# Reordering the last two sequences of a token router, and routing the last one by halves, in a two-layer state-space, attention and mixture-of-experts kernel

## The chip, the cores and the metric

The kernel runs on one NeuronCore of a Trainium2 chip, in one launch. The metric is the device time of that launch in microseconds (us). TensorE (PE) does the matrix products and writes PSUM; its weight loads are shown apart (PEld). VectorE (DVE) and ScalarE (ACT) do elementwise work and reductions, GpSimd (POOL) constants and indirect transfers. Each engine runs its own instructions in order and waits on semaphores of the others. Transfers are issued from the queues of SyncE (SP), ACT and POOL.

## The reference, cut to what matters

The input `x` holds 8 sequences of 1024 tokens with 256 features. Two layers follow each other, each of the form `x = x + attention(norm(x)) + ffn(norm(x))`. The first attention is a state-space scan followed by a layer norm, a GELU and an output projection; the first feed-forward part is a grouped top-2 mixture of experts. The second layer is what the change touches:

```python
qkv = einsum('bsd,fd->bsf', x, w_qkv)          # one head
attention = softmax(attn_logits, axis=1)       # over an axis of length 1
out = einsum(attention, v) @ w_o.T             # so: sum of all tokens' values, for each sequence

logits = xt @ wg                               # 8192 tokens, 8 experts
topv, topi = top_k(softmax(logits), 2)
locs = cumsum(one_hot(topi.T)) - 1             # place of each choice in its expert, all first choices first
valid = pos < capacity                         # capacity 2048
disp[e, pos] += token                          # 8 experts: 256 -> 1024 -> 256, relu
out = sum(gate * y[topi, pos])
```

The place of a token in its expert depends on all tokens before it (and, for second choices, on all first choices), so the routing is a running count over the sequences, and no expert can start before the last token is routed.

## The kernel before, in words

P is 128. A tile is 128 tokens, a sequence is TPB = 8 tiles, NB = 8 sequences, NT = 64 tiles. The state-space scan and the first experts fill the first half of the launch. What is edited is the stage behind it, between the scan and the second layer's experts. For each sequence `b` it does this:

- `project` (L1012, L1019): 16 products per sequence on PE, in four PSUM tiles `pd` of two tiles each, and four additions on DVE of the residual `hb`. The result is the layer's output `y`, which goes to `out_dram` by an SP transfer (L1274) and is later added to there.
- `measure` (L178, L179): mean and variance of each tile on DVE. `roots` (L1030) or, for the last sequence, `scales` (L183 to L185): a square root on ACT, a reciprocal and a product on DVE.
- `normal_out` (L190): eight ACT instructions write the normalised rows `xs`. `normal_in` and `turn` (L933, L934) do the same for the scan output of the next sequence.
- `turn_out` (L1058, L1061): 16 transposes on PE into `pt` (three buffers), and four ACT copies to `xT`, which also sum the tokens into `sums`.
- `logits` (L1069, L1077, L1084, L1085): `xs` goes to the DRAM table `xd`, PE multiplies `xT` with the router weights, ACT copies the logits.
- `attend` (L1092 to L1099): the sum over the tokens times the folded value and output weights, one product pair into the single PSUM bank `pc`.
- `route` for `n` tiles at once (L1106 to L1197): maximum, exponential (ACT, L1112), two picks on DVE (`pick_two`, L200 to L214), counts by two PE products into `pc` (L1120), ACT copies `tot` (L1125), a running sum (L1128), places (L1138 to L1155), and then for both choices and each eight tiles one-hot matrices `hl` and `hh` on DVE (L1161, L1166, L1170), a scaling by the tile number on ACT for each tile (L1174) and a product on PE for each tile (L1176), which adds token numbers up in `pi[0]` and `pi[1]` over the whole launch. At the end the gate weights `w` go to `xd` (L1194).

Sequences are routed in pairs (16 tiles) up to 4 and 5, behind the step of the sequence after them; sequence 6 and sequence 7 are routed alone (8 tiles each). `ends` carries the running count from one `route` to the next.

Behind the last `route`, DVE turns `pi` into the list `invi` (L1327 to L1358), which says for each expert which rows of `xd` it takes. The experts (L1360 on) gather these rows with POOL (L1385), transpose them (L1399), do two products (L1416, L1434) and scatter with addition (L1446).

The source order is not the order of execution: a scheduler interleaves independent instructions of an engine when the program is built. Pools with few buffers (`pc` one, `pt` three, `pd` two, one-hot tiles two) add waits where a buffer is still in use.

Of the kernel before, what the change touches and what calls it, by code (L numbers as in the profile page):

```python
# [24 lines left out]
def kernel(  # L25
# [886 lines left out]
    with tc.tile_pool(name="xr", bufs=3) as xr, tc.tile_pool(name="tr", bufs=1) as tr, tc.tile_pool(  # L912
# [153 lines left out]
        def logits(b):  # L1066

            xs, xT, sums = moved[b][3:]
            nc.sync.dma_start(  # L1069
                xd[b * S : (b + 1) * S, :D].rearrange("(i p) d -> p i d", p=P), xs  # L1070
            )
            pr = ps_d.tile([P, 2, D], F32, name="pd")
            pr = pr.rearrange("p a d -> p (a d)").rearrange("p (t e) -> p t e", t=TPB)
            for t in range(TPB):
                n = 2 if t < TPB - 1 else 1
                for c in range(DC):
                    nc.tensor.matmul(  # L1077
                        pr[:, t : t + n, :],
                        lhsT=xT[:, c, t * P : (t + 1) * P],
                        rhs=wg_t[:, c, : n * (P // 2)],  # L1080
                        start=(c == 0),
                        stop=(c == DC - 1),
                    )
            nc.scalar.copy(logit[:, b % 2 * TPB : (b % 2 + 1) * TPB, :], pr[:, :, :E])  # L1084
            nc.vector.tensor_reduce(colsum[:, :, b], sums, AX.X, ALU.add)  # L1085
# [15 lines left out]
        def route(t0, n, last):  # L1101
# [54 lines left out]

            for j in range(2):
                for i in range(0, n, TPB):
                    some = slice(i, i + TPB)
                    hl = hotp.tile([P, TPB, P], BF16, name="hl")  # L1160
                    nc.vector.tensor_tensor(  # L1161
                        hl, bc(place, 1, [P, TPB, P]), bc(cutb[:, j, some], 2, [P, TPB, P]),
                        ALU.is_equal,
                    )
                    hh = hotp.tile([P, TPB, 2, P], BF16, name="hh")
                    nc.vector.tensor_tensor(  # L1166
                        hh[:, :, 1, :], bc(column[:, j, :], 1, [P, TPB, P]),
                        bc(cutf[:, j, some], 2, [P, TPB, P]), ALU.is_equal,
# [4 lines left out]
                    for t in range(TPB):  # L1173
                        nc.scalar.mul(hh[:, t, 1, :], hh[:, t, 1, :], float(t0 + i + t))  # L1174
                    for t in range(TPB):
                        nc.tensor.matmul(  # L1176
                            pi[j], lhsT=hl[:, t, :], rhs=hh[:, t],
                            start=(t0 + i + t == 0), stop=(t0 + i + t == NT - 1),
                        )
# [74 lines left out]
        for n in (TPB, 2 * TPB):  # L1254
            go_on[n] = r1.tile([P, 2, E, n + 1], F32, name=f"go_on{n}")
            nc.gpsimd.memset(go_on[n], 1.0)
            nc.gpsimd.memset(go_on[n][:, :, :, 0], 0.0)
# [12 lines left out]
        for b in range(NB):  # L1270
# [17 lines left out]
            if b < NB - 1:  # L1288
                measure(b, whole)
                if b:  # L1290
                    logits(last)
                roots(b)
                if b == 0:
                    add_first(1, firsts[1])
                    third = later_rows(2)
                if b == 1:
                    add_first(2, third)
            else:
                measure(b, slice(0, TPB // 2))
                logits(last)  # L1300
# [7 lines left out]
        b = NB - 1  # L1308
        mv, rstd, off = moved[b]
        for some in (slice(0, TPB // 2), slice(TPB // 2, TPB)):  # L1310
            if some.start:
                measure(b, some)
            scales(mv[:, 0, some], rstd[:, 0, some], off[:, 0, some])
            normal_out(b, some)
            turn_out(b, some)
            if not some.start:
                ends = route((b - 1) * TPB, TPB, ends)
        logits(b)
# [3 lines left out]
        ends = route(b * TPB, TPB, ends)  # L1322
# [172 lines left out]
```

## Time and profile before

The median of three runs is 1945.62 us (1943.92 to 1947.21). The profiled execution took 1946.52 us, and its span, from the first to the last instruction, 1944.8 us.

| engine | busy us of 1944.8 | share |
|---|---|---|
| PE | 1806.0 | 93% |
| PEld | 1369.1 | 70% |
| DVE | 707.8 | 36% |
| ACT | 715.4 | 37% |
| POOL | 668.0 | 34% |

A share of the whole span says little on a stage of 60 us in it. Between 952.8 and 1007.8 us, the stage of the last two sequences, DVE is the busy engine. The instructions of that stretch are read from the timeline of each engine, in which a line has the start, the duration and what the engine waited for; durations of neighbours overlap a little there, so the distance from start to start is the better measure of what an instruction costs. [...]

### The profile page before, as it was taken

To read this page: it belongs to the slowest core of one execution; us is meant where nothing else is said; L and a number is where in the kernel's file an instruction comes from. 1 tells how busy PE (TensorE), PEld (TensorE's weight loads), DVE (VectorE), ACT (ScalarE), POOL (GpSimd) and SP (SyncE) were. 2 spreads that over 40 slices of the span, in tenths; PEclk is the share of its full clock that TensorE was granted. 3 is DMA by queue.
4 is the path that set the end of the run, shared out by engine and by line. 5 is a ranking of instruction groups with operands and counts; after the bars stand their busy time and mean duration, and the time that the engine had idled before them with its cause. 6 is when DMAs were issued, how large, how long until landed. Compare 5 with 4: busy or idle time off the path is not lost.

```text
span 1944.8 us, 24219 instructions
## 1 busy us (share of the span) xinstructions
PE 1806.0 (93%) x8619; PEld 1369.1 (70%) x8619; DVE 707.8 (36%) x2121; ACT 715.4 (37%) x1625; POOL 668.0 (34%) x676
## 2 busy tenths in 40 slices
PE   6987789999999998789959999999999999999996
PEld 5876667788888887579836676667667666766764
DVE  6754688354454444687760010101001010100100
ACT  5972354233333321588932222222222222222221
POOL 0100001566666667111013344343333333333322
PEclk9987899899999999899969999999999999999998
DMA  9998422465556566699633465542323232232211
GB/s 267 231 190 178 106 61 83 120 187 161 175 177 174 164 185 190 217 303 230 164 114 55 64 123 80 102 63 61 63 34 82 39 77 41 61 61 35 39 17 22
DMA packets 226840, 233.16 MB, mean 120 GB/s; under 512 B 50904, under 2 KB 199200, under 8 KB 226592
## 3 DMA queue, kind: packets, MB, share of 16 engines
q0 software_dynamic: 65248, 98.68, 26.2%
q1 hardware_dynamic: 158784, 130.54, 23.5%
q10 hardware_dynamic: 2688, 2.40, 0.4%
q8 instruction: 68, 1.11, 0.2%
q14 instruction: 52, 0.43, 0.1%
HBM read 136.87 MB, written 97.85 MB: 121 GB/s over the span
## 4 chain that ended last, share of the span: by engine, by line
PE 52%; DVE 3%; ACT 2%; DMA 1%; issue 1%; POOL 0%; POOLq 0%; ACTq 0%; DVEq 0%
PE phe L1416 23%; PE poe L1434 22%; PE pd L1012 2%; PE px L1399 1%; PE pt L933 1%; PE pd L1077 1%; ACT y L190 1%; DMA out_dram<-yo,invi 1%; DVE st L178 1%; PE pi L1176 1%; DVE hb L977 0%; PE pt L1058 0%; ACT hh L1174 0%; DVE hl L1161 0%; PE pt L1220 0%
## 5 line engine op out<-in xcount | busy, mean ns | idle before, releaser
L1416 PE MATMUL phe<-xTe,w1t 128*128 128x512 f32 x1024 | 447.1, 595 | 0.6 <-DVE xTe L1400 0.6
L1434 PE MATMUL poe<-w2t,hT 128*128 128x256 f32 x2048 | 447.3, 379 | 0.0
L1434 PEld LDWEIGHTS poe<-w2t,hT 128*128 128x128 f32 x2048 | 386.9, 190 | 51.5 <-issue 0.5
L1416 PEld LDWEIGHTS phe<-xTe,w1t 128*128 128x128 f32 x1024 | 195.5, 191 | 233.5 <-issue 230.4
L1446 POOL DMA_INDIRECT out_dram<-yo,invi x128 | 201.8, 1576 | 446.0 <-DMA out_dram<-yo,invi 229.7
L1423 ACT ACTIVATE hT<-phe,b1T 128x512 f32<-128x512 f32 x256 | 175.9, 687 | 248.4 <-PE phe L1416 244.6
L1445 ACT ACTIVATE yo<-yo,gr 128x256 f32<-128x256 f32 x128 | 58.0, 500 | 441.4 <-DVE yo L1441 441.4
L1441 DVE TENSOR_TENSOR yo<-poe,b2t 128x512 f32<-128x512 f32 x64 | 44.2, 691 | 406.6 <-PE poe L1434 406.6
L1385 POOL DMA_INDIRECT xg<-xd,invi x128 | 124.5, 973 | 195.5 <-PE px L1399 90.2
L1400 DVE COPY xTe<-px 128x512 f32<-128x512 f32 x64 | 41.2, 686 | 383.5 <-PE px L1399 383.5
L814 POOL DMA_INDIRECT yr<-yo,goes x142 | 140.3, 988 | 65.6 <-DVE yo L811 27.7
L792 POOL DMA_INDIRECT xb<-xnd,choice x142 | 140.7, 991 | 46.9 <-issue 32.9
L322 PE MATMUL pk<-kr 128*128 128x129 f32 (+7 forms) x896 | 144.7, 298 | 9.7 <-ACT kr L333 9.0
L322 PEld LDWEIGHTS pk<-kr 128*128 128x128 f32 x896 | 125.2, 196 | 30.9 <-ACT kr L333 19.6
L263 PE MATMUL pgu<-xT,wb 128*128 128x256 f32 x568 | 142.2, 394 | 1.0 <-ACT xT L253 0.7
L263 PEld LDWEIGHTS pgu<-xT,wb 128*128 128x128 f32 x568 | 107.8, 196 | 27.6 <-ACT xT L253 13.2
L333 ACT COPY kr<-pk 128x256 f32<-128x256 f32 x192 | 70.0, 373 | 91.5 <-DVE kr L329 88.9
L268 ACT ACTIVATE sg<-pgu 128x256 f32<-128x256 f32 x87 | 33.3, 383 | 186.1 <-PE pgu L263 186.1
L278 PE MATMUL pd<-wb,hh 128*128 128x256 f32 x284 | 80.9, 399 | 5.5 <-DVE hh L271 5.4
L270 DVE TENSOR_TENSOR hh<-pgu,sg 128x256 f32<-128x256 f32 x87 | 36.8, 423 | 133.6 <-ACT sg L268 133.3
L811 DVE TENSOR_SCALAR yo<-pd,xb 128x256 f32<-128x256 f32 x142 | 62.4, 478 | 55.6 <-PE pd L278 54.5
L655 POOL DMA_DIRECT2D base<-y x8 | 12.7, 1582 | 192.8 <-ACT kr L333 56.2
(323 smaller groups left out, 2375.1 us busy)
## 6 DMA issues: line engine op xcount, KB each, us to landing
wb<-wpk SPq DMA_DIRECT2D x71, 384.0 KB, 3.5
xnd<-xr SPq DMA_DIRECT2D x32, 512.0 KB, 8.9
hk<-kscr SPq DMA_DIRECT2D x32, 512.0 KB, 4.7
hb<-yr POOLq DMA_DIRECT2D x10, 1024.0 KB, 12.1
base<-bout_t SPq DMA_DIRECT2D x8, 1024.0 KB, 7.8
base<-y POOLq DMA_DIRECT2D x8, 1024.0 KB, 9.8
hb<-base SPq DMA_DIRECT2D x8, 1024.0 KB, 14.2
out_dram<-y SPq DMA_DIRECT2D x8, 1024.0 KB, 11.5
```

Source lines behind the costliest of these rows:

```text
L263: nc.tensor.matmul(pgu[:, j, :], lhsT=gu[:, j, c, :], rhs=xT[:, c, :], start=(c == 0), stop=(c == DC - 1),)
L278: nc.tensor.matmul(pd[:, q, :], lhsT=hh[:, q * P : (q + 1) * P], rhs=wb[:, 2 * DC * I : WW], start=True, stop=True,)
L322: nc.tensor.matmul(pk[:, j, :n], lhsT=t[:, 1 - j, P:], rhs=t[:, j, P - k : P - k + n], start=True, stop=True,)
L333: nc.scalar.copy(t[:, :, P:], pk[:, :, k : k + P])
L792: nc.gpsimd.indirect_dma_start(out=xb[:, q, : D + 1], out_offset=None, in_=xnd[:, :], in_offset=bass.IndirectOffsetOnAxis(ap=choice[:, 2 * ...
L811: nc.vector.tensor_scalar(yo[:, q, :], pd[:, q, :], xb[:, q, D : D + 1], None, ALU.mult)
L814: nc.gpsimd.indirect_dma_start(out=next(yr_own)[:, :], out_offset=bass.IndirectOffsetOnAxis(ap=goes[:, 2 * n + q : 2 * n + q + 1], axis=0) ...
L1385: nc.gpsimd.indirect_dma_start(out=xg[:, q, :], out_offset=None, in_=xd[:, :], in_offset=bass.IndirectOffsetOnAxis(ap=invi[:, q0 + q : q0 ...
L1416: nc.tensor.matmul(ph, lhsT=w1t[:, c, h * P : (h + 1) * P], rhs=xT[:, c], start=(c == 0), stop=(c == DC - 1),)
L1423: nc.scalar.activation(hT[:, h], ph, AF.Relu, bias=b1T[:, e * HC + h : e * HC + h + 1])
L1434: nc.tensor.matmul(po[:, r, :], lhsT=hT[:, h, q + r, :], rhs=w2t[:, h, :], start=(h == 0), stop=(h == HC - 1),)
L1446: nc.gpsimd.indirect_dma_start(out=of[:, :], out_offset=bass.IndirectOffsetOnAxis(ap=invi[:, q0 + r : q0 + r + 1], axis=0), in_=yo[:, r, : ...
```

## The change

The loop over the sequences now ends at the last but one. Sequence 6 is normalised, transposed and given its logits before the last sequence is projected; it is then routed, and its attention term is made, before the last sequence is measured. The last sequence is measured and normalised in two halves of four tiles, and then each half is transposed, given logits and routed by itself (`route` with four tiles), the second half with the running count of the first. `logits` takes a range of tiles and writes that range of `xd`; `route` builds its one-hot tiles with a width `w` of four or eight. A constant tile for a running sum over four tiles is added.

```diff
@@ -1063,16 +1063,15 @@
                         AF.Copy, accum_out=sums[:, c, hf : hf + 1],
                     )
 
-        def logits(b):
+        def logits(b, some):
 
             xs, xT, sums = moved[b][3:]
-            nc.sync.dma_start(
-                xd[b * S : (b + 1) * S, :D].rearrange("(i p) d -> p i d", p=P), xs
-            )
+            rows = xd[(b * TPB + some.start) * P : (b * TPB + some.stop) * P, :D]
+            nc.sync.dma_start(rows.rearrange("(i p) d -> p i d", p=P), xs[:, some, :])
             pr = ps_d.tile([P, 2, D], F32, name="pd")
             pr = pr.rearrange("p a d -> p (a d)").rearrange("p (t e) -> p t e", t=TPB)
-            for t in range(TPB):
-                n = 2 if t < TPB - 1 else 1
+            for t in range(some.start, some.stop):
+                n = 2 if t < some.stop - 1 else 1
                 for c in range(DC):
                     nc.tensor.matmul(
                         pr[:, t : t + n, :],
@@ -1081,8 +1080,10 @@
                         start=(c == 0),
                         stop=(c == DC - 1),
                     )
-            nc.scalar.copy(logit[:, b % 2 * TPB : (b % 2 + 1) * TPB, :], pr[:, :, :E])
-            nc.vector.tensor_reduce(colsum[:, :, b], sums, AX.X, ALU.add)
+            t0 = b % 2 * TPB
+            nc.scalar.copy(logit[:, t0 + some.start : t0 + some.stop, :], pr[:, some, :E])
+            if some.stop == TPB:
+                nc.vector.tensor_reduce(colsum[:, :, b], sums, AX.X, ALU.add)
 
         def attend(b):
 
@@ -1154,25 +1155,26 @@
             cutf = rt.tile([P, 2, n], F32, name="cutf")
             nc.vector.tensor_copy(cutf, cut[:, 1])
 
+            w = min(n, TPB)
             for j in range(2):
-                for i in range(0, n, TPB):
-                    some = slice(i, i + TPB)
-                    hl = hotp.tile([P, TPB, P], BF16, name="hl")
+                for i in range(0, n, w):
+                    some = slice(i, i + w)
+                    hl = hotp.tile([P, TPB, P], BF16, name="hl")[:, :w]
                     nc.vector.tensor_tensor(
-                        hl, bc(place, 1, [P, TPB, P]), bc(cutb[:, j, some], 2, [P, TPB, P]),
+                        hl, bc(place, 1, [P, w, P]), bc(cutb[:, j, some], 2, [P, w, P]),
                         ALU.is_equal,
                     )
-                    hh = hotp.tile([P, TPB, 2, P], BF16, name="hh")
+                    hh = hotp.tile([P, TPB, 2, P], BF16, name="hh")[:, :w]
                     nc.vector.tensor_tensor(
-                        hh[:, :, 1, :], bc(column[:, j, :], 1, [P, TPB, P]),
-                        bc(cutf[:, j, some], 2, [P, TPB, P]), ALU.is_equal,
+                        hh[:, :, 1, :], bc(column[:, j, :], 1, [P, w, P]),
+                        bc(cutf[:, j, some], 2, [P, w, P]), ALU.is_equal,
                     )
                     nc.vector.tensor_scalar(
                         hh[:, :, 0, :], hh[:, :, 1, :], tokid[:, 0:1], None, ALU.mult
                     )
-                    for t in range(TPB):
+                    for t in range(w):
                         nc.scalar.mul(hh[:, t, 1, :], hh[:, t, 1, :], float(t0 + i + t))
-                    for t in range(TPB):
+                    for t in range(w):
                         nc.tensor.matmul(
                             pi[j], lhsT=hl[:, t, :], rhs=hh[:, t],
                             start=(t0 + i + t == 0), stop=(t0 + i + t == NT - 1),
@@ -1251,7 +1253,7 @@
         nc.gpsimd.memset(sign[:, 0, :], 1.0)
         nc.gpsimd.memset(sign[:, 1, :], -1.0)
         go_on = {}
-        for n in (TPB, 2 * TPB):
+        for n in (TPB // 2, TPB, 2 * TPB):
             go_on[n] = r1.tile([P, 2, E, n + 1], F32, name=f"go_on{n}")
             nc.gpsimd.memset(go_on[n], 1.0)
             nc.gpsimd.memset(go_on[n][:, :, :, 0], 0.0)
@@ -1267,7 +1269,7 @@
         ends = offset
         early = []
         whole = slice(0, TPB)
-        for b in range(NB):
+        for b in range(NB - 1):
             project(b)
             if b < NB - 3:
                 load(b + 3)
@@ -1285,19 +1287,15 @@
                 turn_out(last, whole)
             if b + 1 < NB:
                 turn(b + 1)
-            if b < NB - 1:
-                measure(b, whole)
-                if b:
-                    logits(last)
-                roots(b)
-                if b == 0:
-                    add_first(1, firsts[1])
-                    third = later_rows(2)
-                if b == 1:
-                    add_first(2, third)
-            else:
-                measure(b, slice(0, TPB // 2))
-                logits(last)
+            measure(b, whole)
+            if b:
+                logits(last, whole)
+            roots(b)
+            if b == 0:
+                add_first(1, firsts[1])
+                third = later_rows(2)
+            if b == 1:
+                add_first(2, third)
             if b:
                 attend(last)
             if b and last % 2 == 1:
@@ -1306,20 +1304,29 @@
                 early.append(first_weights(b - NB + 4))
 
         b = NB - 1
+        normal_out(b - 1, whole)
+        turn_out(b - 1, whole)
+        logits(b - 1, whole)
+        project(b)
+        nc.sync.dma_start(
+            of[b * S : (b + 1) * S, :].rearrange("(i p) d -> p i d", p=P),
+            y[:, b * TPB : (b + 1) * TPB, :],
+        )
+        ends = route((b - 1) * TPB, TPB, ends)
+        attend(b - 1)
         mv, rstd, off = moved[b]
-        for some in (slice(0, TPB // 2), slice(TPB // 2, TPB)):
-            if some.start:
-                measure(b, some)
+        halves = (slice(0, TPB // 2), slice(TPB // 2, TPB))
+        for some in halves:
+            measure(b, some)
             scales(mv[:, 0, some], rstd[:, 0, some], off[:, 0, some])
             normal_out(b, some)
+        ready = rt.tile([P, 1], F32, name="ready")
+
+        nc.scalar.activation(ready, rstd[:, 0, TPB - 1 :], AF.Exp, scale=0.0)
+        for some in halves:
             turn_out(b, some)
-            if not some.start:
-                ends = route((b - 1) * TPB, TPB, ends)
-        logits(b)
-        ready = rt.tile([P, 1], F32, name="ready")
-
-        nc.scalar.activation(ready, rstd[:, 0, TPB - 1 :], AF.Exp, scale=0.0)
-        ends = route(b * TPB, TPB, ends)
+            logits(b, some)
+            ends = route(b * TPB + some.start, TPB // 2, ends)
         attend(b)
```

More of the change, by code (lines that the diff above doesn't have):

```diff
@@ L1308 @@
         b = NB - 1
+        normal_out(b - 1, whole)
[8 more added lines that the diff above has]
+        attend(b - 1)
         mv, rstd, off = moved[b]
-        for some in (slice(0, TPB // 2), slice(TPB // 2, TPB)):
-            if some.start:
-                measure(b, some)
+        halves = (slice(0, TPB // 2), slice(TPB // 2, TPB))
+        for some in halves:
+            measure(b, some)
             scales(mv[:, 0, some], rstd[:, 0, some], off[:, 0, some])
             normal_out(b, some)
-            turn_out(b, some)
-            if not some.start:
-                ends = route((b - 1) * TPB, TPB, ends)
-        logits(b)
         ready = rt.tile([P, 1], F32, name="ready")
         nc.scalar.activation(ready, rstd[:, 0, TPB - 1 :], AF.Exp, scale=0.0)
-        ends = route(b * TPB, TPB, ends)
+        for some in halves:
+            turn_out(b, some)
+            logits(b, some)
+            ends = route(b * TPB + some.start, TPB // 2, ends)
         attend(b)
```

## The prediction

> **What bounds the kernel now.** I read the page's chain first, then the waits and the stretches between the last scan result and the first expert.
>
> ```profile
> PE 52%; DVE 3%; ACT 2%; DMA 1%; issue 1%; POOL 0%; POOLq 0%; ACTq 0%; DVEq 0%
> ```
>
> From 1016.7 us on TensorE runs the experts without a gap; that stage (928 us) is not edited and merely starts earlier or later. It starts when `invi` (L1358) is ready: the gathers on POOL follow it. So the question is only when VectorE finishes `invi`, at 1007.77 here. Who is busy until then (columns: window, length, busy us of PE, PEld, DVE, ACT, POOL, clock, DMA share, GB/s):
>
> ```profile
> 952.80:967.70 14.90, 14.73 (x94) 13.35 (x93) 12.54 (x57) 12.06 (x29) 0.00 (x0) 1.00 0.48 146
> 967.70:979.40 11.70, 10.21 (x57) 6.84 (x56) 11.63 (x20) 10.65 (x39) 0.00 (x0) 0.90 0.25 87
> 979.40:988.90 9.50, 5.18 (x30) 3.76 (x29) 7.48 (x46) 2.44 (x13) 0.00 (x0) 0.86 0.82 269
> 988.90:1002.40 13.50, 6.16 (x27) 4.07 (x28) 13.40 (x29) 5.71 (x27) 0.00 (x0) 0.63 0.20 56
> ```
>
> VectorE (third busy figure) is full: 11.63 of 11.70 and 13.40 of 13.50 us. All its waits from 952.8 to 1007.8 are these:
>
> ```profile
> DVE y L1019 <- PE pd L1012: 1.8, 1, 1.8
> DVE token L1339 <- PE pi L1176: 1.7, 2, 1.0
> DVE mx L1108 <- ACT logit L1084: 1.4, 1, 1.4
> DVE rstd L184 <- ACT rstd L183: 0.4, 1, 0.4
> ```
>
> The reader is to see that 5.3 us is all that a better order could win, and that instructions added to VectorE add to the end.
>
> **Prices.** From the groups of VectorE in this stretch:
>
> ```profile
> L1161 DVE TENSOR_TENSOR hl<-place,cutb 128x1024 bf16<-128x1024 bf16 x8 | 9.8, 1221 | 0.0
> L1166 DVE TENSOR_TENSOR hh<-column,cutf 128x1024 bf16<-128x1024 f32 x8 | 9.7, 1218 | 0.0
> L1170 DVE TENSOR_SCALAR hh<-hh,tokid 128x1024 bf16<-128x1024 bf16 x8 | 3.8, 478 | 0.0
> L178 DVE BATCH_NORM_STATS2 st<-y 128x6 f32<-128x256 f32 x8 | 3.2, 400 | 0.0
> ```
>
> Queued starts in the timeline are closer than the durations: 1.14, 1.14, 0.40 and 0.32 us apart, so eight tiles' one-hot work (4 wide, 2 scalings) is 5.33 us. A small instruction that needs the one before it starts 0.32 us later at 16 tiles (L1108 to L1110 at 952.20 and 952.52), 0.255 at 8 (L205 to L206 at 983.34 and 983.59), and 0.21 at 16 elements. For 4 tiles I estimate 0.22, on the line through these. A scan to its first one-hot (L1128 to L1161) took 3.16 us at 16 tiles (964.60 to 967.76) and 2.29 at 8 (986.58 to 988.87). Half a one-hot block holds 512 elements instead of 1024: 0.60, 0.60 and 0.26 us, so 2.9 us per four tiles (estimates: half of 1.14 or 0.40 with the fixed part kept).
>
> **The change, part by part.** Call the routing of sequences 4 and 5 R45, of 6 R6, of the last R7a and R7b. The built programs have the same VectorE order up to 952.81 (L1110 of R45) and the same ScalarE order up to the last `xs` of sequence 6 (957.49).
>
> 1. Sequence 6 turned ahead of the last projection. TensorE no longer projects at 952.84 to 959.75; the transposes wait for `xs`. R45's exponential still ends at 955.04. VectorE, free of the four residual additions (0.6 us each) and of eight statistics that sat in this pick, does the pick alone: ten steps of 0.32 from 955.1 and 0.28 for the last, hots at 958.7 instead of 961.6. Counting matmuls take 1.09 us (961.68 to 962.77), done 959.9; the count copies no longer sit behind the square root's table load (1.28 us), done 960.3 instead of 964.6. First one-hot of R45 at 960.34 + 3.16 = 963.5 instead of 967.8: a head start of 4.3 us. The projection follows the router matmuls at about 963.8.
>
> 2. What that displaces. R45's one-hot work is 10.7 us, three additions go in or behind it (1.8): 963.5 + 12.5 = 976.0. The fourth needs TensorE's last projection matmul, which stands behind R45's last products and so behind ScalarE's scalings (to 977.2): ready 978.0. Eight statistics (0.32 and 0.09) interleave with R6's pick. First scale and offset 981.4; ScalarE writes four `xs` (0.51 each) to 983.55, and only then the second half's square root, on which VectorE waits from 983.2 to 983.9. R6's scan starts at 984.2, its one-hot at 986.5 (before: 988.9). Head start left: 2.4 us.
>
> 3. R6's one-hot work: 986.5 to 991.85. In the old kernel the last sequence's pick (L1108 at 981.33 to L1193 at 986.43) was already done by then and the last scan stood inside this block; here nothing of R7 has begun. A chain of cross waits begins instead: attention's matmul holds the single `pc` bank until R6's ranks are read (985.5), the last `xs` are written at 987.9, three `xT` at 989.7, then ScalarE's queue has eight scalings (0.21 apart) that wait for VectorE until 990.4 and end at 992.1, and the logit copy of R7a is behind them: VectorE waits 0.4 us. The exponential is behind eight more (to 993.95): pick of R7a from 994.25, a wait of 1.5 us.
>
> 4. R7 by halves. R7a: 12 dependent steps of 0.22 and three more, a wait for the sums of the fourth `xT`, to the hots at 996.9; counting and copies 1.05 us (1.33 at 8 tiles, from 982.61 to 983.94), scan at 998.0, one-hot at 1000.45 (1.95 us of chain, step by step; the line through 3.16 and 2.29 would give 1.86; and 0.5 of R7b's first steps between), to 1003.5 with one step between. R7b: its pick goes on to 1004.9, counts 1005.9, ranks and the `taken` work (3.0 us for 8 tiles, 993.81 to 996.82; 2.5 here) to 1008.45, one-hot to 1011.4.
>
> 5. The end. Before, from the start of the last scaling (1001.88) to `invi` 5.89 us, of which eight ScalarE scalings took 1.71; with four it is 0.85 less, the scaling itself 0.15: 1011.1 + 4.85 = 1015.9.
>
> **Sum:** 1015.9 - 1007.8 = 8.1 us later. A ledger agrees: the second pick, count and rank adds about 4.3 us, smaller one-hot blocks 0.5, waits go from 3.6 (5.3 without those for `token`) to 6.7 (2.3 for R45's exponential, 0.75 for its count copies, then 0.7, 0.4 and 1.5 as in 2 and 3, 0.8 for R7's counts, 0.25 elsewhere), the end gives back 1.0; that is 6.9, and the rest (1.2) is small gaps that interleaved work had filled.
>
> **Costed at nothing:** the split row write and the split `xs` write on SP. The last `w` is ready near 1005.6 and such writes landed 6.0 us after issue at the least; 1011.6 is ahead of `invi`. The median of all five was 10.2 and the longest 14.4, which would cost 0 to 4 us; at a quarter of the largest one's packets, with `w2t` (issued near 992.6) past, I take 6.0. SP carries both `w2t` loads ahead of the half writes; their first use is 14 us after the experts start. The `b1`, `b2` issues on ScalarE's queue (0.52 and 0.60 us) fall into its idle time at 995. POOL has no work here; one more pair of memsets on it lies far ahead. The last projection's result is now written out (L1274, 1 MB) at about 979 instead of 960.5: on SP it stands behind R45's row write, and holds up nothing, since the next in SP's queue, R6's rows, are ready at 983; who waits for its landing (11.5 us at the median) is the last attention copy into `y`, near 1006. Sequence 6's `xs` write keeps its place at 957.5. TensorE idles around 953 to 957 for want of `xs`; only the projection is late by it, and that is in 2.
>
> [...]
>
> **Rivals.** [...] Chance 0.14. (b) Faster: the 4.3 us head start of step 1 reaches the end and the end is 1.0 shorter, 5.3 us: 1940.3. It decides if VectorE has over 8 us to spare between 976 and 1000. The profile shows 2.0 us of it to spare between 979.4 and 988.9 and 0.1 behind. Chance 0.06. (c) The last row write lands late and the gathers wait, or TensorE's clock, 0.63 in the last stretch, falls further and slows counts and products: 3 to 5 us more, to 1958. Chance 0.12. (d) The order is in effect inert, within 0.2%: as (a) with all waits hidden, chance 0.06. The walk itself, 0.62.
>
> **How the numbers follow.** The profiled execution took 1946.5 us (span 1944.8); with the shift 1954.6. Against the median of 1945.6, which is 0.9 below it: 1953.7. Its own range, with 2.5 us of error in some 200 steps and the spread of 1.6 of the runs, is 1950.7 to 1956.7. To hold eight in ten: 1948.5 to 1957.5. 0.2% is 3.9 us, about what a measurement of this kernel can tell from none: the borders are 1941.7 and 1949.5. Faster 0.06; within 0.2% 0.10; slower 0.84.
>
> **What would show it.** In the changed profile R45's first one-hot should start near 963.5, R6's near 986.5, the first half's exponential near 994, `invi` end near 1016, VectorE's waits name the logit copy and the copy or square root of ScalarE. Step 1 is wrong if the first is later than 966; steps 3 and 4 are wrong if R7a's pick starts before 990; the whole is wrong if `invi` ends before 1008, or if the experts' 928 us changes.

## The result, and the profile after

The changed kernel takes 1953.21 us (median of ten runs, 1948.46 to 1957.23) against 1944.84 us before (ten runs, 1941.11 to 1947.25): a ratio of 1.0048, with a 95% interval from 1.0036 to 1.006, or 7.0 to 11.7 us slower. The profiled execution took 1953.18 us, its span 1951.5 us, at a granted clock of 0.962 as before.

One measure serves for all kernels below. The *stretch* runs on VectorE from the first `mx` of sequences 4 and 5 (L1108, after L1109) to the end of `invi`. It is 952.20 to 1007.77 = 55.57 us before and 950.65 to 1014.88 = 64.23 us after: 8.66 us longer. The span grew by 6.7 us only, because in the execution after, the stretch began 1.55 us earlier (nothing in front of it is edited) and the rest behind `invi` took 936.6 instead of 937.0 us. To set a time of the profile after against one of the prediction, add 1.55.

The chain of waits on the page after, in answer to the one shown before:

```profile
PE 47%; DVE 1%; DMA 1%; issue 0%; POOL 0%; ACT 0%; POOLq 0%; ACTq 0%; DVEq 0%
```

It still consists of the experts on TensorE; the view could not have sized the change, since a stage of 60 us is 3% of the span. VectorE's waits from 951 to 1015:

```profile
DVE vals L203 <- ACT pr L1113: 3.6, 2, 2.3
DVE cum L1129 <- ACT tot L1126: 2.9, 3, 1.7
DVE token L1346 <- PE pi L1178: 0.9, 2, 0.5
DVE rstd L184 <- ACT rstd L183: 0.7, 1, 0.7
DVE mx L1109 <- ACT logit L1084: 0.2, 1, 0.2
```

That is 8.3 us in place of 5.3. The wait for `pd` (1.8 us) is gone and the one for `logit` is short; in their place VectorE waits for the exponential and for the counts. By stage, from one first one-hot to the next (columns as in the prediction):

```profile
951.25:962.94 11.69, 9.00 (x54) 6.96 (x52) 7.27 (x32) 7.41 (x19) 0.00 (x0) 0.85 0.36 97
962.94:976.90 13.96, 11.56 (x63) 8.26 (x63) 13.93 (x22) 7.18 (x34) 0.00 (x0) 1.00 0.00 0
976.90:985.65 8.75, 4.81 (x20) 3.81 (x18) 7.71 (x46) 6.43 (x13) 0.00 (x0) 0.68 0.57 184
985.65:991.40 5.75, 4.81 (x33) 3.72 (x32) 5.51 (x7) 4.92 (x20) 0.00 (x0) 0.89 0.26 93
991.40:998.79 7.39, 4.37 (x32) 3.27 (x31) 5.28 (x38) 2.91 (x16) 0.00 (x0) 1.00 0.90 282
998.79:1007.09 8.30, 4.45 (x16) 3.05 (x16) 7.13 (x36) 2.09 (x10) 0.00 (x0) 0.60 0.42 137
1007.09:1014.88 7.79, 2.92 (x11) 1.13 (x9) 6.49 (x22) 2.40 (x10) 0.00 (x0) 0.50 0.00 0
```

VectorE is full only in the one-hot stages (second and fourth row). In the picks around them (first, third, fifth and sixth) it stands idle for 1.0 to 4.4 us each. The two picks of the last sequence, 7.39 and 8.30 us, come after all one-hot work of the others. Some marks in VectorE's timeline (start, duration, what it waited for):

```profile
959.76 0.72 DVE L1129 TENSOR_TENSOR_SCAN cum<-go_on,tot 128x272 f32<-128x272 f32 x1 [1.65 <-ACT tot L1126]
...
993.17 0.19 DVE L203 TENSOR_REDUCE vals<-pr 128x4 f32<-128x32 f32 x1 [1.31 <-ACT pr L1113]
993.39 0.19 DVE L205 TENSOR_TENSOR cand<-pr,vals 128x32 f32<-128x32 f32 x1
...
998.79 0.68 DVE L1163 TENSOR_TENSOR hl<-place,cutb 128x512 bf16<-128x512 bf16 x1
999.39 0.69 DVE L1168 TENSOR_TENSOR hh<-column,cutf 128x512 bf16<-128x512 f32 x1
...
1014.59 0.29 DVE L1365 TENSOR_TENSOR invi<-token,second 128x128 int32<-128x128 f32 x1
```

### The profile page after: what moved, and what is told of

Its sections match the earlier page's. It is cut to its first block, busy times and chain, and to the rows that moved or that the text cites. A ratio compares the mean times of both kernels' runs of the same rounds, so it can differ in the third digit from the quotient of the medians.

```text
span 1951.5 us, 24275 instructions
## 1 busy us (share of the span) xinstructions
PE 1805.5 (93%) x8623; PEld 1366.8 (70%) x8623; DVE 712.5 (37%) x2157; ACT 716.4 (37%) x1629; POOL 668.4 (34%) x678
## 5 line engine op out<-in xcount | busy, mean ns | idle before, releaser
L811 DVE TENSOR_SCALAR yo<-pd,xb 128x256 f32<-128x256 f32 x142 | 62.5, 479 | 55.4 <-PE pd L278 55.1
```

Of the source, the lines that this page charges most:

```text
L811: nc.vector.tensor_scalar(yo[:, q, :], pd[:, q, :], xb[:, q, D : D + 1], None, ALU.mult)
```

## The experiments

The question behind them was not the size, which the walk had, but its cause: the prediction's ledger puts most of it on the halves. Ten kernels take the change apart. The kernel before took 1943.23 us on the chip of e1 to e4, and 2023.61 to 2025.90 us on the chips of the other six, the difference lying in the work ahead of this stage; so stretches are compared between kernels, and launch times only with the runs of the kernel before on the same chip.

Each stretch is read from one execution, so it matters how well an execution repeats. Where two kernels have the same order of instructions (before and e2 for the first 27 us of the stretch; after, e1, e3 and e5 for the first 38), VectorE's starts agree to 0.03 us. Before and g3 are an exception, and it comes from TensorE's granted clock. These two have the same order on VectorE, ScalarE and TensorE for the first 35 us. Their times agree to 0.02 us up to TensorE's router products for the last sequence, of which these are the first ten, in before and then in g3 (whose stretch begins at 1034.13):

```profile
976.70 2.65 PE L1077 MATMUL pd<-wg_t,xT 128*128 128x128 f32 x10 [0.67 <-ACT xT L1061]
```

```profile
1058.61 1.74 PE L1077 MATMUL pd<-wg_t,xT 128*128 128x128 f32 x10 [0.67 <-ACT xT L1061]
```

The granted clock in the 4.5 us around them was 0.62 in before (from 976.5) and 1.00 in g3 (from 1058.43). VectorE's wait of 1.44 us for the last logits stands in before and is gone in g3, which is 1.5 us ahead from there on. So a difference of about 2 us or less between two stretches is not settled by them alone unless the clock followed the same course; one of 6 us and more is.

All times in this table are from VectorE's timeline, in us from the first `mx` of the stretch. "Idle" is the time in it that no VectorE instruction covers, "summed" the sum of all their durations, which overlap a little. The launch ratio has its 95% interval.

| kernel | R45 one-hot | R6 one-hot | last `mx` | last one-hot | end | idle | instructions, summed | launch ratio |
|---|---|---|---|---|---|---|---|---|
| before | 15.6 | 36.7 | 29.1 | 44.6 | 55.6 | 6.6 | 162, 58.8 | 1 |
| after | 12.3 | 35.0 | 40.8 | 48.1, 56.4 | 64.2 | 10.3 | 198, 64.7 | 1.0048 (1.0036 to 1.006) |
| e1, reordered, last one whole | 12.3 | 35.0 | 46.8 | 54.8 | 65.9 | 15.4 | 162, 58.9 | 1.0051 (1.0033 to 1.0069) |
| e2, halves in the old order | 15.6 | 34.5 | 27.5 | 41.9, 49.7 | 57.5 | 6.6 | 198, 63.8 | 1.0013 (0.9999 to 1.0027) |
| e3, quarters | 12.3 | 35.0 | 41.0 | 51.4 to 64.2 | 70.3 | 11.6 | 270, 75.4 | 1.0076 (1.0057 to 1.0095) |
| e4, change but projection first | 15.6 | 33.8 | 29.1 | 45.5, 49.8 | 57.6 | 6.1 | 198, 64.1 | 1.0006 (0.9993 to 1.002) |
| e6, projection moved alone | 12.3 | 36.6 | 42.4 | 51.4 | 62.5 | 11.1 | 162, 59.1 | 1.0062 (1.0038 to 1.0087) |
| e7, early routing of 6 alone | 15.6 | 34.3 | 32.1 | 45.8 | 56.9 | 8.2 | 162, 58.9 | 1.0021 (0.9996 to 1.0045) |
| e5, after with 6 scaled on GpSimd | 12.3 | 35.0 | 40.5 | 49.7, 58.0 | 65.8 | 9.3 | 198, 67.2 | 1.0044 (1.0022 to 1.0065) |
| g1, before with gates on GpSimd | 14.2 | 31.9 | 36.8 | 46.6 | 57.7 | 10.1 | 150, 55.9 | 1.0002 (0.998 to 1.0024) |
| g2, g1 and three scalings on ScalarE | 14.2 | 32.0 | 36.5 | 45.8 | 56.1 | 9.7 | 147, 54.5 | 0.9991 (0.9971 to 1.0012) |
| g3, three scalings on ScalarE | 15.6 | 35.2 | 27.6 | 42.5 | 53.2 | 5.3 | 159, 57.2 | 0.9991 (0.9963 to 1.0018) |

"Last `mx`" is the first of the last sequence; for halves, "last one-hot" gives both. e1, e6 and e7 have the instructions of before, to within 0.3 us of their sum, and take 1.3 to 10.3 us more. What differs is the order, and in part TensorE's clock.

### The two halves of the change: e1 and e2

```diff
 # e1, on the kernel after
         for some in halves:
             turn_out(b, some)
-            logits(b, some)
-            ends = route(b * TPB + some.start, TPB // 2, ends)
+        logits(b, whole)
+        ends = route(b * TPB, TPB, ends)
```

> The changed kernel with one thing put back: the last sequence is given logits and routed whole (8 tiles), so only the reordering is left. I measure the stretch on VectorE from the first maximum of the pair of sequences 4 and 5 to the end of invi: 55.6 us in the kernel before, 64.2 in the changed one. Theory (VectorE is full; the reordering ends with the last sequence's pick standing alone behind sequence 6's one-hot work, and the halves add a further chain): 60 to 62.5 us, so 4.5 to 7 us slower than before. Rival A (the reordering is a gain, its 4.3 us head start lasts, and the halves cost everything): 50.5 to 52 us, faster than before by 4. Rival B (the reordering costs everything, the halves nothing): 64 us.

Measured: 1955.23 us against 1943.23, stretch 65.86 us, above all three forecasts. With the last sequence whole, the reordering took 10.3 us over before, 1.6 more than with the halves. VectorE waits for the last logits longer than for anything else in the stretch:

```profile
997.44 0.21 ACT L1084 COPY logit<-pd 128x64 f32<-128x64 f32 x1 [3.57 <-PE pd L1076]
997.69 0.22 DVE L1109 TENSOR_REDUCE mx<-logit 128x8 f32<-128x64 f32 x1 [5.99 <-ACT logit L1084]
```

The first line is ScalarE's timeline, the second VectorE's. After a wait of 5.99 us the pick of eight tiles follows with no work of another sequence beside it: first one-hot at 54.78, 8.0 us later.

Not all of that wait belongs to the order. In e1 TensorE's clock was 0.50 from 988 to 994, while it made these logits; in after it was 1.00. The order of the two kernels parts at 37.3 us of the stretch, and the clocks had parted half a microsecond or more before. The same number of router products in e1 and in after:

```profile
989.76 3.19 PE L1076 MATMUL pd<-wg_t,xT 128*128 128x128 f32 x14
```

```profile
993.77 1.77 PE L1076 MATMUL pd<-wg_t,xT 128*128 128x128 f32 x14 [0.42 <-ACT xT L1061]
```

At after's clock e1's logits would have come some 2 us earlier (an estimate: 1.4 us from these products, 0.7 from the nine after them). So the 1.6 us in favour of the halves may be the clock's; the launches, 1.0051 and 1.0048, do not tell the two kernels apart.

```diff
 # e2, on the kernel before (with the functions of after)
-        logits(b)
         ...
-        ends = route(b * TPB, TPB, ends)
+        for some in (slice(0, TPB // 2), slice(TPB // 2, TPB)):
+            logits(b, some)
+            ends = route(b * TPB + some.start, TPB // 2, ends)
```

> The kernel before with the other part alone: the order stays, but the last sequence's logits and routing are done in two halves of 4 tiles. Stretch as for the run above. Theory (a second pick, count and rank of small dependent instructions adds about 4.8 us to a full VectorE, the shorter end gives 1.0 back, waits may add a little): 59 to 61 us, 3.5 to 5.5 us slower than before. Rival A (halves cost everything): 64 us or more. Rival B (halves cost nothing): 55 to 56 us.

Measured: 1947.05 us, stretch 57.53 us, 2.0 us over before, where the theory had 3.5 to 5.5. TensorE's clock followed nearly the same course in both up to 41 us (the ten router products shown above took 2.55 us in e2 and 2.65 in before). VectorE carries 36 instructions more, 5.0 us of durations, and its idle time did not change (6.6 us). VectorE's timeline in e2 shows why they are cheap there:

```profile
985.47 0.17 DVE L213 SCALAR_TENSOR_TENSOR rest<-hots,pr 128x32 f32<-128x32 f32 x1
985.58 0.17 DVE L1127 COPY tot<-cum 128x16 f32<-128x16 f32 x1
985.66 0.28 DVE L1144 TENSOR_TENSOR at__9541<-at__9541,hots 128x128 f32<-128x128 f32 x1
985.86 0.17 DVE L203 TENSOR_REDUCE vals<-rest 128x4 f32<-128x32 f32 x1
985.96 0.17 DVE L1187 TENSOR_TENSOR w<-hots,vals 128x32 f32<-128x32 f32 x1
```

The pick of the first half (`rest`, `vals`, `w`) and the ranks of sequence 6 (`tot`, `at`) take turns. A small instruction of 32 elements is followed by the next after 0.10 to 0.11 us; the next is of another chain. In the profile after, `vals` and `cand` of the same size stand 0.22 us apart (993.17 and 993.39).

### Each further split: e3

```diff
 # on the kernel after
             turn_out(b, some)
-            logits(b, some)
-            ends = route(b * TPB + some.start, TPB // 2, ends)
+            for q in (slice(some.start, some.start + 2), slice(some.start + 2, some.stop)):
+                logits(b, q)
+                ends = route(b * TPB + q.start, TPB // 4, ends)
```

> The changed kernel with the suspected cost doubled: the last sequence is routed in four parts of 2 tiles. Theory (each further part is one more chain of about 30 dependent small instructions, a count on TensorE and two copies, about 5 us each beside the one-hot work): stretch 72 to 75 us, 8 to 11 us over the changed kernel. Rival (what costs is the reordering, a further split hides behind the one-hot work): 64 to 66 us.

Measured: 1959.79 us, stretch 70.31 us: 6.1 us over after for two further splits, about 3.0 each, with 36 more instructions each. That is under the theory and over the rival, and between e2's 2.0 and the 4.8 us of the ledger. TensorE's clock was half for some 5 us longer here than in after (0.60 and 0.50 there in the last two stages), which may have a part in it.

### The place of the projection: e4, e6 and e7

```diff
 # e4, on the kernel after
+        project(b)
+        nc.sync.dma_start(of[...], y[...])
         normal_out(b - 1, whole)
         turn_out(b - 1, whole)
         logits(b - 1, whole)
-        project(b)
-        nc.sync.dma_start(of[...], y[...])
```

> The changed kernel with the last projection put back ahead of the turning of sequence 6, as it was before; sequence 6 is still routed before the last sequence is measured, and the last still by halves. Theory (the late projection pushes four additions and eight statistics behind the one-hot work of the pair, and the last rows with them; early, they fill the gaps of the pair's pick, at the cost of the head start): 60 to 63 us. Rival (the position of the projection does not matter, since VectorE's sum of work is the same): 64 us.

Measured: 1946.47 us, stretch 57.63 us, under the theory's 60 to 63 and far from the rival's 64. All of the change except the projection's place took 2.1 us, and its place the other 6.6.

```diff
 # e6, on the kernel before; the same three calls leave their old places for b = NB - 1
+            if b == NB - 1:
+                normal_out(b - 1, whole)
+                turn_out(b - 1, whole)
+                logits(b - 1)
             project(b)
```

> The kernel before with one thing of the change alone: sequence 6 is normalised, turned and given its logits ahead of the last projection; it is still routed where it was, and the last sequence whole. The runs so far gave stretches of 55.6 (before), 57.5 (halves only), 57.6 (all of the change but the projection's position) and 65.9 (reordering with the last whole). New theory (the position of the projection is what costs: additions, statistics and rows of the last sequence come 12 to 18 us later, so its pick no longer overlaps anything): 63.5 to 66, 8 to 10 us slower than before. Rival (it costs only together with the early routing of sequence 6): 55.5 to 58.

Measured: 2036.47 us against 2025.90, stretch 62.52 us: 7.0 us, a little under the new theory and far above the rival. (The launch interval, 7.7 to 17.6 us, lies a little higher; the 1.5 us that before lost to the clock, and e6 did not, may be a part of that.) Cut at the first one-hot of each routing, the stretch has four stages: 15.6, 21.1, 8.0 and 11.0 us before, and 12.3, 24.3, 14.9 and 11.1 us in e6. The second and third of them, before and then in e6, in the view of busy times by stage:

```profile
967.76:988.87 21.11, 15.30 (x85) 10.54 (x82) 19.02 (x63) 13.02 (x51) 0.00 (x0) 0.88 0.51 168
988.87:996.82 7.95, 3.62 (x18) 2.38 (x18) 7.92 (x24) 3.74 (x18) 0.00 (x0) 0.50 0.35 97
```

```profile
1029.89:1054.17 24.28, 19.32 (x97) 14.46 (x97) 22.59 (x68) 17.64 (x55) 0.00 (x0) 0.86 0.14 45
1054.17:1069.03 14.86, 9.72 (x52) 6.59 (x51) 12.08 (x44) 6.27 (x26) 0.00 (x0) 0.84 0.84 283
```

VectorE's instruction counts (in brackets, third) tell the story. In the first stage they fall from 58 to 32: the last projection's additions and statistics have left it, and it is 3.3 us shorter. They are done in the second stage, which loses the last pick to the third; it has 5 instructions more and is 3.2 us longer, as they no longer fill the gaps of a pick. The third has 20 more and is 6.9 us longer. In the old order the last pick ran in the second stage, beside the pick of sequence 6. Here it starts 42.4 us into the stretch, behind the one-hot work, and stands alone in VectorE's timeline:

```profile
1059.98 0.22 DVE L1108 TENSOR_REDUCE mx<-logit 128x8 f32<-128x64 f32 x1
...
1061.73 0.22 DVE L203 TENSOR_REDUCE vals<-pr 128x8 f32<-128x64 f32 x1 [1.27 <-ACT pr L1112]
...
1066.28 0.46 DVE L1128 TENSOR_TENSOR_SCAN cum<-go_on,tot 128x144 f32<-128x144 f32 x1 [0.96 <-ACT tot L1125]
```

9.05 us from maximum to one-hot (1069.03), with two waits for other engines (2.2 us) and steps 0.26 us apart.

Three pairs of kernels differ in the projection's place alone: before and e6, e4 and after, e7 and e1. The late place is longer in each, by 7.0, 6.6 and 9.0 us of stretch, and in the launch ratios by 1 to 1.0062, 1.0006 to 1.0048 and 1.0021 to 1.0051.

```diff
 # e7, e4 with the last sequence whole
             turn_out(b, some)
-            logits(b, some)
-            ends = route(b * TPB + some.start, TPB // 2, ends)
+        logits(b, whole)
+        ends = route(b * TPB, TPB, ends)
```

> Edit: the projection of the last sequence first, as in the kernel before; sequence 6 turned and routed ahead of the last sequence's measuring, as in the changed kernel; the last sequence whole. It completes the square of the two parts other than the projection's place. Known stretches (first maximum of sequences 4 and 5 to the end of invi): before 55.6, halves alone in the old order 57.5 (+2.0), early routing of 6 and halves 57.6 (+2.1), whole change 64.2, whole change but the last undivided 65.9 (so halves gave 1.6 back there). Theory I (the halves pay only where the last pick would otherwise stand alone behind all one-hot work): early routing alone costs what the halves then give back, so the stretch is 59.2 or more, some 3.7 us over before, and the third maximum comes behind sequence 6's one-hot work. Theory II (the parts add, and early routing costs nothing while the projection is first): 55.5 to 56, no different from before. Launch: ratio 1.0015 to 1.002 by theory I, 1.000 by theory II.

Measured: stretch 56.88 us, 1.3 us over before, ratio 1.0021 with an interval that includes 1. Neither theory has it: theory I asked for 3.7 or more, theory II for 0.4 or less. The last `mx` came at 32.1, ahead of sequence 6's one-hot work at 34.3, so with the projection first the two picks still overlap. The clock was half at other times than in before (0.50 there from 36.7 to 44.6 us), so 1.3 us is not clear of it, nor is the way in which early routing (1.3) and halves (2.0) add up to 2.1 in e4. With the projection late, early routing took 10.3 (e1) less 7.0 (e6), 3.3 us, of which some 2 may be e1's clock.

### Two suspected waits and spare work: e5, g1, g2 and g3

```diff
 # e5, on the kernel after
-                    for t in range(w):
-                        nc.scalar.mul(hh[:, t, 1, :], hh[:, t, 1, :], float(t0 + i + t))
+                    if t0 == (NB - 2) * TPB:
+                        nc.gpsimd.tensor_tensor(hh[:, :, 1, :], hh[:, :, 1, :],
+                            bc(tileno[:, t0 : t0 + w], 2, [P, w, P]), ALU.mult)
+                    else:
+                        for t in range(w):
+                            nc.scalar.mul(hh[:, t, 1, :], hh[:, t, 1, :], float(t0 + i + t))
```

> The changed kernel with one queue relieved: the 16 scalings of sequence 6's one-hot tiles by their tile numbers are taken from ScalarE and done by two GpSimd products with a constant. Stretch on VectorE from the pair's first maximum to the end of invi, 64.2 us in the changed kernel. Theory (the first half's logit copy and exponential stand behind these scalings on ScalarE; VectorE's waits of 0.2 and 1.3 us for them go): 62.5 to 63.2. Rival (the last rows themselves come too late, so the wait moves to the copies of xT and the logits): 64 or more.

Measured: stretch 65.77 us, 1.5 us longer than after, with TensorE's clock on the same course (VectorE's waits for the counts of the two halves are 0.38 and 0.90 us in both). That is the rival's number, but not its cause. The wait for the exponential (1.31 us) is gone, and nothing is won: two VectorE instructions beside GpSimd's products took 1.0 and 1.7 us more. From VectorE's and GpSimd's timelines:

```profile
1069.59 1.22 DVE L1168 TENSOR_TENSOR hh<-column,cutf 128x1024 bf16<-128x1024 f32 x1
...
1071.40 1.45 DVE L1172 TENSOR_SCALAR hh<-hh,tokid 128x1024 bf16<-128x1024 bf16 x1
...
1073.05 1.99 DVE L1093 COPY vb<-colsum 128x256 f32<-128x256 f32 x1
```

```profile
1069.82 2.75 POOL L1176 TENSOR_TENSOR hh<-hh,tileno 128x1024 bf16<-128x1024 bf16 x1 [58.94 <-issue]
1072.99 1.90 POOL L1176 TENSOR_TENSOR hh<-hh,tileno 128x1024 bf16<-128x1024 bf16 x1 [0.43 <-DVE pr L1111]
```

Elsewhere the last two VectorE instructions take 0.48 and 0.28 us. So e5 leaves open what the ScalarE queue alone costs; it moved the delay to another place.

```diff
 # g1, on the kernel before: the four products and sums of w
-            nc.vector.tensor_tensor(w, w, bc(sm, 2, full), ALU.mult)
+            nc.gpsimd.tensor_tensor(w, w, bc(sm, 2, full), ALU.mult)
             ...
```

> The kernel before with four instructions of each routing step taken off VectorE: the gate weights (lines 1185 to 1193 of it: two products, a sum, a product) are made by GpSimd, which has no work here. If VectorE's sum of work sets the end, the last three routing steps give back 12 instructions of 0.14 to 0.32 us, some of which only fill gaps: stretch 53.5 to 54.8, 1 to 2 us faster. Rival (dependent chains set it, these instructions only fill their gaps): 55.3 to 55.8.

Measured: stretch 57.70 us, 2.1 us longer than before with 2.9 us less work on VectorE, against both forecasts; launch ratio 1.0002. From 35 us on, TensorE's clock stayed at half here and did not in before (0.81 in its last stage), which may be a part of the 2.1. The scheduler's order turned with the edit: sequence 6 got to its one-hot work 4.8 us earlier (31.9), and the last pick fell behind it (36.8). In VectorE's timeline:

```profile
1073.54 0.21 DVE L1108 TENSOR_REDUCE mx<-logit 128x8 f32<-128x64 f32 x1
...
1076.07 0.22 DVE L203 TENSOR_REDUCE vals<-pr 128x8 f32<-128x64 f32 x1 [1.78 <-ACT pr L1112]
...
1080.60 0.46 DVE L1128 TENSOR_TENSOR_SCAN cum<-go_on,tot 128x144 f32<-128x144 f32 x1 [1.73 <-ACT tot L1125]
```

It is e6's picture in a kernel that has nothing of the change: the last pick alone, 9.8 us from maximum to one-hot.

```diff
 # g3, on the kernel before; g2 is g1 with this edit
-                    nc.vector.tensor_scalar(
-                        hh[:, :, 0, :], hh[:, :, 1, :], tokid[:, 0:1], None, ALU.mult)
+                    if t0 >= (NB - 2) * TPB and (t0, j) != ((NB - 1) * TPB, 1):
+                        nc.scalar.mul(hh[:, :, 0, :], hh[:, :, 1, :], tokid[:, 0:1])
+                    else:
+                        nc.vector.tensor_scalar(
+                            hh[:, :, 0, :], hh[:, :, 1, :], tokid[:, 0:1], None, ALU.mult)
```

> As the run before, and for the one-hot blocks of sequence 6 and the first of sequence 7 the scaling by the token number (0.40 us each on VectorE) is one ScalarE instruction of about 1.1 us ahead of the tile scalings. If VectorE's work sets the end: 1.2 us less again, stretch 52.3 to 53.6. Rival (ScalarE's products then come too late for the tile buffers): no gain over the run before.

Measured: stretch 56.13 us, 1.6 us less than g1 (1.2 forecast), but far from the 52.3 to 53.6 that was built on g1's forecast; ratio 0.9991. ScalarE's two instructions took 1.15 and 1.13 us.

> Edit, on the kernel before: of the last four one-hot blocks (both of sequence 6, both of the last), the first three have their scaling by the token number (L1170, one VectorE instruction of 1024 elements, 0.40 us from start to start) as one ScalarE instruction (1.15 us in the run that had this edit together with the gate weights on GpSimd). That run's stretch was 1.6 us shorter than that of the gate weights alone. Theory I (the order and the cover decide; the scaling lies on the way of the last products, ScalarE's instruction starts as soon as hh is there and delays nothing, and no other dependent chain loses its cover): 1.2 us of VectorE's work off, stretch 54.0 to 54.6 against 55.6. Theory II (ScalarE's queue then holds the exponential or the tile-number scalings of the last block, a wait in place of the work): 55.6 or more, with a wait for pr or pi that grew by 1 us. Launch: ratio 0.9993 or 1.0000, less than the interval.

Measured: stretch 53.17 us, 2.4 us under before and the shortest of all, where theory I had 1.0 to 1.6. But 1.5 of it is the clock: it is there at the last logits, ahead of any edited block. What is left for the edit is 0.9 us, a little under theory I. In the launch it can't be told from no change: 0.9991, interval 0.9963 to 1.0018.

## Why the prediction was right, and where its account was not

**The size.** 1953.7 us was forecast and 1953.21 measured; 8.1 us in the stretch and 8.66 measured. The walk earned that, since its steps held one by one, to within 1.0 us; the ledger's agreement with it was in part luck.

**Step 1.** The exponential ended at 955.04 in the prediction's time and the second `hots` at 958.68, as walked. The mis-sized term is the counts: 1.09 us taken over from the old kernel, 2.0 here. TensorE had stood waiting for `xs` (it was busy 3.31 of the 6.00 us from 951), and its granted clock in the next 3 us was 0.57 where it had been 1.00 (window 957 to 960, and its counting products in TensorE's timeline):

```profile
957.00:960.00 3.00, 3.00 (x14) 2.41 (x13) 1.25 (x5) 1.37 (x6) 0.00 (x0) 0.57 1.01 328
```

```profile
957.26 1.14 PE L1121 MATMUL pc<-hots,before 128*128 128x256 f32 x2
958.20 1.06 PE L1121 MATMUL pc<-hots,ones 128*128 128x256 f32 x2
```

It is the late projection that brings this. In all five kernels that have it (after, e1, e3, e5, e6) TensorE was busy 3.3 to 3.6 of those 6 us, and the clock in the next 3 us was 0.50 to 0.58; in the other seven it was busy all 6 us, and the clock was 1.00. So VectorE waited 1.65 us for `tot`, not 0.75, and R45's one-hot work began at 964.5, not 963.5. That TensorE's idling cost the projection alone ("only the projection is late by it") was wrong by this 1.0 us.

**Steps 2 to 5.** In the prediction's time, forecast and measured: R6's one-hot 986.5 and 987.2, with the wait for the square root at 0.7 and 0.70; the logit wait 0.4 and 0.25, the exponential's 1.5 and 1.31; R7a's `vals` 994.25 and 994.7, its one-hot 1000.45 and 1000.3, R7b's 1008.45 and 1008.6; steps of 0.22 and half blocks of 0.60 as estimated; from the last scaling (1009.89) to the end of `invi` 4.85 (its terms give 4.89) and 4.99; the end 1015.9 and 1016.4. The writes called hidden were: POOL began its first gather 0.88 us after `invi`, as it did before.

**The ledger.** As a sum it held. VectorE's covered time grew by 8.66 - 3.77 = 4.9 us (4.8 were forecast for the second pick and the small blocks, less the little that the end gives back on VectorE). Its named waits without those for `token` went from 3.6 to 7.4 (6.7 forecast), and those for `token` fell by 0.8. Its 4.3 for the second pick, count and rank was the author's estimate, and no run shows it: at the prediction's step times some 30 split instructions would give 30 x (2 x 0.22 - 0.255) = 5.6, and in e2 the halves cost 2.0.

As an account of causes it failed. By it, leaving the halves out would win 3.8 us (4.8 less 1.0). e1, which leaves them out, was 1.6 us longer, and would still not be more than about half a microsecond shorter if some 2 us of it are the clock's. The halves took 2.0 us in the old order; in the new one they added 3.4 us of covered time and took 5.1 of idle, and whether they cost or win there is open. What costs is the projection's place: 6.6, 7.0 and 9.0 us in the three pairs, the last with e1's clock in it.

**The premise that failed** is that VectorE, covered for 13.40 of 13.50 us, is full, and so "that instructions added to VectorE add to the end". A chain of small dependent instructions looks busy, 0.19 us of duration in each 0.22, but another chain could have run inside it: e2 put in 36 instructions of 5.0 us for 2.0 us more of covered time and none of idle, and g1 took 2.9 us of instructions out and won nothing. VectorE's work was neither what set the end nor free; how much of it had other work beside it counts as well. "5.3 us is all that a better order could win" was reasoned in the same way: it took the covered time as fixed, and the same 162 instructions cover 48.7 us of the stretch in e7 and 51.4 in e6.

**What a row measures.** The 0.22 us for 32 elements is the distance of a step to the one it depends on, as in after (993.17 to 993.39); e2's interleaved steps of that size stand 0.10 to 0.11 apart, each 0.17 us long. So a step's price read from a chain is not what the engine has to give for it where another chain runs beside. Why the two distances differ no run isolates.

**The rivals.** Halves that cost less because steps hide behind each other are what e2 shows, 2.0 us, but in the old order. In the new one R7a's pick stood alone: 7.39 us, of which VectorE was idle for 2.11. (b) had a head start that lasts: it was 3.3 us at R45's one-hot work, 1.7 at R6's, and gone by the last's. Of (c), the row write was in time, and the clock was 0.60 and 0.50 in the last two stages, against 0.50 and 0.81 in the last two of before; where it cost, with 1.0 us, was in step 1. (d) is excluded by the interval.

**Left open.** Why the clock fell in before and not in g3, with the same order. Whether the halves cost or win in the new order, and what early routing costs: no kernel was profiled twice. e5's question, what ScalarE's queue costs the first half's exponential. The effect of the scheduler's order apart from the edits, which g1 mixes.

## What to carry to other kernels

Before work is added to or moved past a stage of many small dependent instructions, ask which independent chain runs beside it and whether it still does afterwards: the same 162 instructions took 55.6 to 65.9 us here (some 2 us of the longest may be TensorE's clock), and the early start that a move wins (3.3 us) counts for nothing if the last chain is left alone (9.05 us). The busy share of the engine was no measure here of what it could still take (13.40 of 13.50 us in before; e2's 36 further instructions, 5.0 us of durations, cost 2.0). A ledger whose sum is right is no proof of its entries: undo one entry at a time. And before a difference of 2 us between two profiled stretches is explained, compare the granted clock in both.

## What the runs showed of the hardware that was not expected

The same instructions in the same order ran TensorE at half clock in one execution and at full clock in another: 0.62 in before and 1.00 in g3 over the same 4.5 us, with ten products in 2.65 and 1.74 us. The granted clock is part of what a single profile measures.

A VectorE scaling of 1024 bf16 elements took 1.45 us instead of 0.48, and a copy of 256 fp32 elements 1.99 instead of 0.28, beside a GpSimd product; they ended 0.28 and 0.15 us after the product did (1072.57 and 1074.89). A comparison that began 0.23 us ahead of the first product (L1168 at 1069.59) kept its 1.22 us; there it was the product that took longer, 2.75 us against 1.90 for the second. g1 has the same: a sum on GpSimd that began inside such a comparison (1020.72, 1.42 us) took 1.33 us, and the same sum 0.45 beside other work. From GpSimd's timeline:

```profile
1021.12 1.33 POOL L1192 TENSOR_TENSOR w<-w,w__8959 128x128 f32<-128x128 f32 x1
...
1046.64 0.45 POOL L1192 TENSOR_TENSOR w<-w,w__9386 128x128 f32<-128x128 f32 x1
```

What holds the two engines up beside each other no run isolates.

Four counting products took 2.0 us at a granted clock of 0.57, against 1.09 us at 1.00, with TensorE busy for 3.31 of the 6.00 us ahead of them. Where a move leaves TensorE waiting, as in the five kernels with the late projection, the next short chain through it should not be priced at the old duration.
